# Nine shared weight buffers, and GpSimd's side work tied to the softmax's low parts

## The chip, the cores and the metric

One core of one Trainium2 chip (trn2). The metric is the device time of one execution in microseconds (us), the median of several runs. Lower is better. Five engines run their own instruction queues in order: TensorE (PE; its weight loads are PEld), VectorE (DVE), ScalarE (ACT), GpSimd (POOL) and SyncE (SP, which here only issues DMAs). They meet through semaphores.

## The reference, cut to what matters

Two layers, each "x + attention(xn) + ffn(xn)" with xn the layernorm of x; x is (2, 1024, 512) in float32.

```python
# layer 0: one head of size 128, softmax over all 1024 keys
attn = softmax(einsum('bqd,bkd->bqk', q, k) * scale);  out = (attn @ v) @ Wo + bo
# layer 0 ffn: 4 streams of 128; H_res = (1-g) I + g * sinkhorn(logits, 50 iterations)
x_mixed = einsum('btij,btjc->btic', H_res, x_streams)
y       = einsum('btnc,btn->btc', x_streams, H_pre) @ W_branch
ffn0    = x_mixed + einsum('btc,btn->btnc', y, H_post)
# layer 1: 32 heads of size 128, 8 shared K/V heads from low-rank latents, causal
q = xn @ Wq.T;  k = (xn @ Wk_down.T) @ Wk_up.T;  v = (xn @ Wv_down.T) @ Wv_up.T
attn1 = (softmax(where(causal, q @ k.T * scale, -1e9)) @ v) @ Wo.T
# layer 1 ffn: a dense product, and a low-rank one weighted by a top-2 gate over 8 experts
ffn1 = xn @ weight.T + (((xn @ lora_A) * w) @ lora_B) / 16
```

## The kernel before, in words

**Numbers.** A float32 operand is scaled and split in two float16 parts, high and low; a product is three passes of matmuls (high by high, high by low, low by high; `mm3`, `attn_out`). Weights come by a DMA that POOL issues (`fetch`) into a float32 staging tile `f2k` (four slots), and `split_pool` makes the parts with three POOL instructions: scale (L94), high part (L95), low part (L96). Products leave PSUM through `evac`: ACT writes the high part (L104), DVE the low part (L105).

**Tiles and slots.** A tile's tag names a ring of slots; a new tile waits until a slot's last reader is done. The tags that matter here: `f2k` (FB = 4), `h2k` (HB = 3), `wo` (WB = 5), `wq` (4), `P` (PB = 3, softmax rows in float32), `Phl` (LB = 3, their two parts), `PT` (3, transposed parts).

**A row step.** Layer 1 works per batch through NG = 8 groups of four heads that share one K/V head; a group has 32 row steps, each of 32 queries by four heads (128 partitions) against `QR * (s + 1)` keys. In a step (`row_step`): PE computes the scores of row s (`rows_scores`); the row before gets its reciprocal (L301) on DVE and its high part (L307) on ACT (`rows_hi`); row s gets its scaled minimum on DVE (L282, L286, the last of which is `last_row`) and its exponential on ACT (L290) (`rows_exp`); then the row before gets its **low part** on DVE (L313), a POOL memset of the part of the 128-block that causality leaves empty (L317), and one transposing DMA into `PT` (`rows_lo`). Three steps later PE multiplies by V (`group_av`), and every fourth step by Wo (`wo_block`, added into `acc` at L729). `Phl` and `P` have three slots, so a transpose that comes late holds up rows.

**What is hung on the row steps.** `layer1_attn` keeps a list `fill[(group, step)]`; `at(g, s, f)` puts work there and `put(h, s, f)` does so for the list `extra`, counted in rows from the start. Per group: K/V weights fetched at step 1 and split at 3; the four Wq weights of the next group fetched at 5, 9, 13, 17 and split two steps later; the four Wo weights of the next group fetched at 33, 35, 37, 39 and split two steps later, which is in steps 1 to 9 of that next group. During the first batch's eight groups, `extra` also holds the second batch's layer 0: its Sinkhorn chain on POOL with reciprocals on DVE (`chain_pool`, one `chain_step` for about each row from 1 to 117), its mix sums (`mix0_units`: a scaling on POOL at L613, four times four ACT scalings at L628, four POOL sums at L629), the branch (`branch0_add`, L449 and L451), its layernorm and transposes, its latents (`lat_w`, `lat_unit`), both batches' gating, and the last layer's weights (`ffn_w`, six weights, fetched and split in one go at row 212, and again at row 466 for the second batch).

**Who sets the order.** The program is traced in this order, and the Tile framework then orders each engine's queue by a simulated timeline: of the instructions that are ready there, the one traced first. Two tools bend it: `tc.issue_after(i)` and `behind(i, j)` add an edge without a semaphore: i is placed after j in the plan, but on the chip nothing waits. In the kernel before, `parts_of` places a split behind `last_row`:

```python
        hl = T(tag, [P, 2, 512], F16, bufs=bufs)
        behind(split_pool(st, hl[:, 0], hl[:, 1], scale), last_row[0])
```

Of the kernel before, what the change touches and what calls it, by code (L numbers as in the profile page):

```python
# [9 lines left out]
F16 = mybir.dt.float16  # L10
F32 = mybir.dt.float32
AF = mybir.ActivationFunctionType
ALU = mybir.AluOpType
# [3 lines left out]
P = 128  # L17
S = 1024
NB = 2
NT = S // P  # L20
# [5 lines left out]
CAPACITY = 768.0  # L26
LN_EPS = 1e-5
RMS_EPS = 1.1920929e-07
FB, HB, PB, LB, XB, WB = 4, 3, 3, 3, 4, 5
QR = 32  # L30
NR = P // QR
LG = ((0, 1, 2, 3), (4, 5, 6, 7))
# [9 lines left out]
G0, G1, GL, WT, LX, LA = 16, 200, 3, 220, 231, 240  # L42
AVD, WOD = 5, 10
KVN, QN, QNN, QH = 19, 18, 24, 1
FW, FF = 212, 221
BS, BP, BV = 4, 3, 1
CQ, CV = (0, 1), (0, 0)
PSCALE = 16384.0
# [3 lines left out]
def tile_model(ctx: ExitStack, tc: tile.TileContext, out: bass.AP, a: dict):  # L52
# [16 lines left out]
    def C(name, shape, dt=F32):  # L69
        return const.tile(shape, dt, tag=name, name=name)  # L70
# [5 lines left out]
    def bc(ap, axis, n):  # L76
        return ap.unsqueeze(axis).to_broadcast(
            [*ap.shape[:axis], n, *ap.shape[axis:]])
# [101 lines left out]


    last_pool, last_row, last_T = [None], [None], [None]
    last_hi, last_lo = [None], [None]

    def after(*insts):

# [2 lines left out]
            st.enter_context(tc.issue_after(i.ins))  # L189
        return st  # L190

    def behind(i, j):

        tc.add_manual_dep(i.ins, j.ins.name, mybir.DependencyInfo(
            mybir.DependencyClass.NoSync, mybir.DependencyReason.DATA), reason="behind")

    def rsqrt(y, ve, tag):

# [24 lines left out]
        return V.scalar_tensor_tensor(rs[:, 1, sl], mv[:, sl, 0], -1.0, rs[:, 2, sl],  # L223
                                      ALU.mult, ALU.mult)

    def normed_T(b, mv, rs, t, dst, pool, tags=(("f2k", FB), ("h2k", HB))):

        xn = T(tags[0][0], [P, NC, P], bufs=tags[0][1])
        xf = xn.rearrange("p c d -> p (c d)")
        hl = T(tags[1][0], [P, NC, 2, P], F16, bufs=tags[1][1])  # L230
        if pool > 1:
            A.activation(xf, acc[b, t], AF.Identity, scale=rs[:, 2, t:t + 1], bias=rs[:, 1, t:t + 1])
        elif pool:
            G.tensor_scalar(xf, acc[b, t], rs[:, 2, t:t + 1], rs[:, 1, t:t + 1], ALU.mult, ALU.add)
        else:
            V.tensor_scalar(xf, acc[b, t], rs[:, 2, t:t + 1], rs[:, 1, t:t + 1], ALU.mult, ALU.add)
        last_hi[0] = A.activation(hl[:, :, 0, :], xn, AF.Copy)
        eng = G if pool in (1, 2) else V
        lo = eng.tensor_tensor(hl[:, :, 1, :], xn, hl[:, :, 0, :], ALU.subtract)
        (last_pool if eng is G else last_lo)[0] = lo  # L240
        last_T[0] = nc.sync.dma_start_transpose(dst, hl.rearrange("p c l d -> p (c l d)"))
# [67 lines left out]
    def rows_lo(Pm, r, W, pool, hl, dst):  # L309
        if pool:  # L310
            G.tensor_tensor(hl[:, 1, :W], Pm[:, :W], hl[:, 0, :W], ALU.subtract)
        else:
            lo = V.scalar_tensor_tensor(hl[:, 1, :W], Pm[:, :W], r[:, 1:2], hl[:, 0, :W],  # L313
                                        ALU.mult, ALU.subtract)
        if W < hl.shape[2]:

            behind(G.memset(hl[:, :, W:], 0.0), lo)  # L317
        nc.sync.dma_start_transpose(dst, hl.rearrange("p l k -> p (l k)"))
# [32 lines left out]
    def front0(b, between=lambda: None):  # L351
        mv, rs = layernorm(b, "a")
        xT = T("xT", [P, NT, 2 * NC, P], F16, bufs=1)
        for ts in F0[b]:
            layernorm_tiles(b, mv, rs, ts)
            for t in ts:
                if b == 0:
                    tags = ("wq", 4), (("h2k", HB), ("wo", WB))[t % 2]
                    normed_T(b, mv, rs, t, xT[:, t], FP[b][t], tags)
                    if t == X1:  # L360
                        with tc.issue_after(last_T[0].ins):
                            load_x(1)
                else:
                    normed_T(b, mv, rs, t, xT[:, t], FP[b][t])
                    between()
            if b == 0 and ts[0] == 0:
                split_w0a()
# [6 lines left out]
        rf = T("rf", [P, NT], bufs=2)  # L374
        rsqrt(rf, ms, "rs")
        V.tensor_scalar(rf, rf, 1.0 / 1024.0, None, ALU.mult)
        lg = C(f"lg{b}", [P, NT, 24])
        Vh = T("V", [P, NT, 2, P], F16, bufs=2)
        for t in range(NT):
            p = PP() if t % 2 or b else srow()  # L380
# [64 lines left out]
    def branch0_add(b, t, y4, hh):  # L445

        y = y4
        y4 = T("f2k", [P, 4, P], bufs=FB)
        G.tensor_tensor(y4, bc(y, 1, 4), bc(hh[:, t, 1, :], 2, P), ALU.mult)  # L449
        af = acc[b, t]  # L450
        G.tensor_tensor(af, af, y4.rearrange("p i c -> p (i c)"), ALU.add)  # L451

# [139 lines left out]
    def mix0_units(b, t, rs, pool):  # L592


        got = {}

        def load():
            if b == 0 and t >= 4:
                if t % 2 == 0:
                    xr_more[t] = T("P", [P, 2, H], bufs=PB)  # L600
                xr = got["xr"] = xr_more[t & ~1][:, t % 2]
            else:
                xr = got["xr"] = T("xr", [P, H], bufs=XB)
            with after(t0):
                nc.sync.dma_start(xr, a["x"][(b * NT + t) * P:(b * NT + t + 1) * P, :])
            if b == 0:
                A.activation(xr, xr, AF.Identity, scale=rs[:, 2, t:t + 1], bias=rs[:, 1, t:t + 1])
                if not pool:
                    got["d"] = srow() if t < 4 else PP()
                    A.activation(got["d"], acc[b, t], AF.Copy)  # L610
                return
            with tc.issue_after(p0.ins):
                G.tensor_scalar(xr, xr, rs[:, 2, t:t + 1], rs[:, 1, t:t + 1], ALU.mult, ALU.add)  # L613

        def stream(j):
            if b == 0 and (not pool or j > 1):
                with after(*(last_rs[:1] if pool else last_rs[1:] if j else last_mix)):
                    stream_at(j)
            else:
                stream_at(j)  # L620

        def stream_at(j):
            xj = got["xr"][:, j * P:(j + 1) * P]
            by = [Hm[b][:, t, i, j:j + 1] for i in range(NC)]
            if pool:
                m = T("f2k", [P, H], bufs=FB)
                for i in range(NC):
                    A.activation(m[:, i * P:(i + 1) * P], xj, AF.Copy, scale=by[i])  # L628
                G.tensor_tensor(acc[b, t], acc[b, t], m, ALU.add)  # L629
                return  # L630

            for i in range(NC):
                sl = slice(i * P, (i + 1) * P)
                dst = acc[b, t] if j == NC - 1 else got["d"]
                last_stt[0] = V.scalar_tensor_tensor(dst[:, sl], xj, by[i], got["d"][:, sl], ALU.mult, ALU.add)

        return [load] + [lambda j=j: stream(j) for j in range(NC)]
# [30 lines left out]
    def lat_w(mc):  # L668
        st = T("f2k", [P, NC, P], bufs=FB)
        nc.gpsimd.dma_start(st, a["Wlat"][mc])  # L670
        w1 = T("h2k", [P, 2, NC, P], F16, bufs=HB)
        split_pool(st, w1[:, 0], w1[:, 1], 32.0)
        return w1

# [4 lines left out]

    def parts_of(st, tag, scale, bufs):  # L680

        hl = T(tag, [P, 2, 512], F16, bufs=bufs)
        behind(split_pool(st, hl[:, 0], hl[:, 1], scale), last_row[0])
        return hl

    def kv(b, g):
# [4 lines left out]
            got["st"] = fetch(a["Wup"][g])  # L691

        def split():
            w = parts_of(got["st"], *(("h2k", 32.0, HB) if g + b else ("wo", 32.0, WB)))
            got["w"] = w.rearrange("p l (s c d) -> p l s c d", s=2, c=2)
            got["K"] = T("K", [P, 2, S], F16, bufs=2)
            got["V"] = T("V", [P, 2, NT, P], F16, bufs=2)
# [60 lines left out]
    def layer1_attn(kv0, start, extra):  # L758
# [5 lines left out]
        def at(g, s, f):  # L764
            g, s = g + s // NS, s % NS
            fill.setdefault((g, s), []).append(f)
# [29 lines left out]
        for g in range(N):  # L796
            if g + 1 < N:
# [8 lines left out]
                for u in range(4):  # L806
                    at(g, QNN + 2 * u if new else QN + 4 * u, lambda g=g, u=u: q_unit(g + 1, u))
                for hh in range(4):
                    at(g, 33 + 2 * hh, lambda g=g, hh=hh: fetch_wo(g + 1, hh))
                    at(g, 35 + 2 * hh, lambda g=g, hh=hh: split_wo(g + 1, hh))  # L810
            for u in range(4):
                at(g, QH + (1 if (g + 1) % NG == 0 else 3) * u, lambda g=g, u=u: q_unit(g, 4 + u))
            for c in range(NT):
# [108 lines left out]

    ffw = {}

    def ffn_w():
        w = T("cmp", [P, 6, 2, H], F16, bufs=1)

        parts = [(a["WmT"][c * P:(c + 1) * P, :], 64.0) for c in range(NC)]
        parts += [(a["loraA"], 4.0), (a["loraB"], 16.0)]
        for k, (src, scale) in enumerate(parts):  # L930
            st = T("f2k", [P, H], bufs=FB)
            nc.gpsimd.dma_start(st, src)
            split_pool(st, w[:, k, 0], w[:, k, 1], scale)
            ffw["ABCDEF"[k]] = w[:, k]

    def ffn_block(b, t):
        xT = xT1[b]
# [50 lines left out]
        xT1[b] = T("xT", [P, NT, 2 * NC, P], F16, bufs=1)  # L988

    def xT_tile(b, t, pool):  # L990
        normed_T(b, *ln1[b], t, xT1[b][:, t], pool, (("f2k", FB), ("h2k", HB)) if b else
                 (("xr", XB), (("h2k", HB), ("wo", WB))[t % 2]))

    def tile_of(b, t):
        d = T("h2k", [P, 2 * NC, P], F16, bufs=HB)
        normed_T(b, *ln1[b], t, d, True, (("f2k", FB), ("xr", XB)))
        return d

# [36 lines left out]
        extra.setdefault((s // (S // QR), s % (S // QR)), []).append(f)  # L1035

    def chain_step():
        with tc.issue_after(last_row[0].ins):
            next(chain, None)

    for k in range(102):
# [36 lines left out]
    for mc in range(4):  # L1078
        put(0, LA + 2 * mc - 4, lambda mc=mc: lw.update({mc: lat_w(mc)}))
        for th in range(2):  # L1080
            put(0, LA + 2 * mc + th, lambda mc=mc, th=th: lat_unit(mc, th))
    put(0, FW, ffn_w)
    put(58, 2, ffn_w)
    for t in range(NT):
        put(0, FF + t, lambda t=t: ffn_block(0, t))
        put(60, 4 * t + 3, lambda t=t: ffn_block(1, t))
# [48 lines left out]
```

## Time and profile before

| | before |
|---|---|
| median of 3 runs | 1868.62 us (1867.13 to 1870.87) |
| the profiled execution, its own time | 1873.71 us |
| its span in the profile | 1871.6 us |
| mean granted TensorE clock | 0.971 |
| PE, DVE, ACT, POOL busy | 1724.0, 1473.9, 1198.8, 900.4 us |
| low parts (L313) | 464.5 us in 515, mean 913 ns |
| POOL memsets (L317) | 75.8 us in 384, mean 207 ns; 414.1 us idle before them for a transpose's landing |
| one Wo split on POOL, means | L94 679, L95 658, L96 1285 ns |

All of it is one execution on the chip. "Busy" is the time in which an engine has an instruction under way; a PE that is busy need not be at its peak. In the timeline a line gives start, length, engine, source line, operation, the tile written and those read, shapes, how many instructions are merged, and in brackets how long the engine was idle before it and what released it. Layer 0 takes about the first 234 us; the first batch's eight groups run from there to about 1100 us, the second batch's to the end.

### The profile page before, as it was taken

Reading aid. Unit: us, or ns where it says so; the run is one execution under the profiler, and the core shown is the slowest. Engines: PE = TensorE matmul, PEld = TensorE weight load, DVE = VectorE, ACT = ScalarE, POOL = GpSimd, SP = SyncE. Lnnn points to the kernel's source line nnn. Section 1 sums busy time; section 2 is a strip of 40 time slices with the busy share of each in tenths; the row PEclk is TensorE's granted clock in tenths of the full one; section 3 lists DMA queues with packets and bytes.
Section 4 is the critical chain, followed back from the end, with each engine's and each line's share of the span. In section 5 each row is a group of like instructions: output and inputs, shape, how many; then the busy total and the mean of one; then the engine's idle time right before and its main releaser. Section 6 shows DMA issues by size and latency. Waiting matters only on the chain. (4 is left out here: it accounts for less than half of the span.)

```text
span 1871.6 us, 34948 instructions
## 1 busy us (share of the span) xinstructions
PE 1724.0 (92%) x11458; PEld 1047.7 (56%) x11458; DVE 1473.9 (79%) x4050; ACT 1198.8 (64%) x2917; POOL 900.4 (48%) x1540
## 2 busy tenths in 40 slices
PE   4756399989999999999999999999999999999998
PEld 3333145656666566566555556566666666655665
DVE  8888977988888878787967767777777878777675
ACT  4747665657666787867535646666676767675554
POOL 5657667576857373727525332334242415155200
PEclk9887699999999999999999999999999999999999
DMA  7425234656554656477538645756565666666456
GB/s 209 91 46 112 76 66 96 149 113 133 129 127 104 150 121 152 99 146 159 134 85 154 124 101 128 131 125 146 115 143 123 137 123 141 118 143 138 89 125 119
DMA packets 707305, 230.25 MB, mean 123 GB/s; under 512 B 689953, under 2 KB 690081, under 8 KB 707122
## 3 DMA queue, kind: packets, MB, share of 16 engines
q1 hardware_dynamic: 691666, 180.75, 47.2%
q0 software_dynamic: 13152, 43.07, 8.6%
q10 hardware_dynamic: 2304, 4.20, 0.7%
q8 instruction: 90, 1.47, 0.3%
q14 instruction: 93, 0.76, 0.1%
HBM read 52.81 MB, written 4.19 MB: 30 GB/s over the span
## 5 line engine op out<-in xcount | busy, mean ns | idle before, releaser
L290 ACT ACTIVATE P<-P,nm 128x1024 f32<-128x1024 f32 (+31 forms) x528 | 391.7, 742 | 261.3 <-DVE nm L282 248.3
L313 DVE SCALAR_TENSOR_TENSOR Phl<-P,r,Phl 128x1024 f16<-128x1024 f32 (+31 forms) x515 | 464.5, 913 | 109.5 <-ACT Phl L307 104.6
L343 PE MATMUL av<-PT,V 128*128 128x256 f16 x3648 | 451.9, 275 | 18.3 <-DMA PT<-Phl 12.7
L88 PE MATMUL s<-K,Q 128*128 128x512 f16 (+22 forms) x2400 | 447.3, 319 | 22.0 <-DVE P L286 16.0
L343 PEld LDWEIGHTS <-V 128*128 128x128 f16 x3648 | 357.6, 99 | 110.4 <-issue 11.6
L307 ACT ACTIVATE Phl<-P,r 128x1024 f16<-128x1024 f32 (+31 forms) x515 | 370.2, 732 | 28.7 <-DMA PT<-Phl 12.6
L88 PE MATMUL pp<-wo,ao 128*128 128x512 f16 x1536 | 373.7, 380 | 4.6 <-ACT ao L104 3.7
L88 PE MATMUL pp<-xT,wq 128*128 128x512 f16 x1536 | 369.3, 380 | 0.9 <-DVE xr L855 0.5
L317 POOL MEMSET Phl<- 128x192 f16 (+2 forms) x384 | 75.8, 207 | 530.5 <-DMA PT<-Phl 414.1
L88 PEld LDWEIGHTS <-Q 128*128 128x128 f16 x2400 | 224.0, 99 | 180.6 <-issue 34.1
L88 PEld LDWEIGHTS <-wq 128*128 128x128 f16 x1536 | 149.6, 98 | 167.5 <-issue 3.0
L88 PEld LDWEIGHTS <-ao 128*128 128x128 f16 x1536 | 149.6, 98 | 155.6 <-ACT ao L104 5.6
L282 DVE CUSTOM_DVE_ANT_0 P<-s,mask,nm 128x272 f32<-128x272 f32 (+15 forms) x256 | 157.4, 616 | 21.2 <-PE s L88 13.3
L286 DVE TENSOR_SCALAR_CACHE_REDUCE P<-s 128x512 f32<-128x512 f32 (+15 forms) x272 | 152.4, 561 | 14.6 <-PE s L88 11.4
L302 ACT ACTIVATE r<-r 128x1 f32<-128x1 f32 x528 | 96.4, 193 | 76.2 <-DVE r L301 76.0
L104 ACT ACTIVATE ao<-av 128x512 f16<-128x512 f32 x128 | 75.4, 589 | 107.2 <-PE av L343 104.0
L301 DVE RECIPROCAL r<-r 128x1 f32<-128x1 f32 x528 | 80.7, 157 | 77.4 <-ACT P L290 73.2
L94 POOL TENSOR_SCALAR f2k<-f2k 128x512 f32<-128x512 f32 x164 | 110.3, 679 | 48.3 <-DMA f2k<-in_Wq 19.3
L729 DVE SCALAR_TENSOR_TENSOR acc<-pp,acc 128x512 f32<-128x512 f32 x128 | 86.8, 678 | 38.3 <-PE pp L88 37.9
L105 DVE SCALAR_TENSOR_TENSOR Q<-pp,Q 128x512 f16<-128x512 f32 x128 | 87.2, 681 | 31.9 <-ACT Q L104 31.8
L282 DVE CUSTOM_DVE_ANT_0 P<-s,mask 128x32 f32<-128x32 f32 (+15 forms) x256 | 104.9, 429 | 8.7 <-PE s L88 8.3
L104 ACT ACTIVATE Q<-pp 128x512 f16<-128x512 f32 x128 | 74.5, 582 | 55.1 <-PE pp L88 53.4
(262 smaller groups left out, 2113.5 us busy)
## 6 DMA issues: line engine op xcount, KB each, us to landing
f2k<-in_Wq POOLq DMA_DIRECT2D x64, 256.0 KB, 3.2
f2k<-in_WoT POOLq DMA_DIRECT2D x64, 256.0 KB, 3.3
PT<-Phl SPq DMA_TRANSPOSE x528, 3.4
acc<-in_x SPq DMA_DIRECT2D x16, 256.0 KB, 4.0
f2k<-in_Wup POOLq DMA_DIRECT2D x16, 256.0 KB, 3.6
out<-acc ACTq DMA_DIRECT2D x16, 256.0 KB, 3.7
xr<-in_x SPq DMA_DIRECT2D x12, 256.0 KB, 3.0
f2k<-in_Wlat POOLq DMA_DIRECT2D x8, 256.0 KB, 5.5
```

The source lines that it names most:

```text
L88: nc.tensor.matmul(dst, lhs(l), rhs(r), start=(i == 0 and j == 0), stop=(i == n - 1 and j == 2))
L94: first = G.tensor_scalar(stage, stage, scale, 1.0, ALU.mult, ALU.mult)
L104: A.activation(hl_hi, src, AF.Copy, scale=scale)
L105: return V.scalar_tensor_tensor(hl_lo, src, scale, hl_hi, ALU.mult, ALU.subtract)
L282: last_row[0] = V.tensor_tensor_reduce(Pm[:, o:o + w], pt[:, :w], mask[:, 512 - w:], -scale, first, ALU.add, ALU.min, nm[:, k:k + 1])
L286: last_row[0] = V.tensor_scalar(Pm[:, o:o + w], pt[:, :w], -scale, first, ALU.mult, ALU.min, accum_out=nm[:, k:k + 1])
L290: A.activation(Pm[:, :W], Pm[:, :W], AF.Exp, bias=last, scale=-1.0, accum_out=r[:, 0:1])
L302: A.activation(r[:, 1:2], r[:, 1:2], AF.Copy, scale=PSCALE)
L307: A.activation(hl[:, 0, :W], Pm[:, :W], AF.Copy, scale=r[:, 1:2])
L313: lo = V.scalar_tensor_tensor(hl[:, 1, :W], Pm[:, :W], r[:, 1:2], hl[:, 0, :W], ALU.mult, ALU.subtract)
L343: nc.tensor.matmul(p, Vh(j, l), PT(r * nj + j), start=(j == 0 and k == 0), stop=(j == nj - 1 and k == 2))
L729: V.scalar_tensor_tensor(acc[b, t], p, 1.0 / 256.0, acc[b, t], ALU.mult, ALU.add)
```

## The change

1. The tag `h2k` goes; its tiles join the tag `wo`, which now has nine slots instead of three and five. The tile `lg`, two constants before, is one slot that both batches share.
2. `last_low` remembers the newest low part on DVE (L313). `behind` can now add a real wait (a semaphore). `parts_of` (the Wq, Wo and K/V splits) uses it: a split's first instruction waits for `last_low`. So do the second batch's scaling, mix sums and branch product on POOL. `chain_step` is placed after `last_low` instead of `last_row`, without a wait.
3. The Wo weights of the next group are split at steps 22, 25, 28, 31 (at the change of batch 26, 28, 30, 32) and fetched two steps before.
4. The last layer's six weights are fetched and split one at a time, two rows apart, from row 210 and from row 466, each split behind `last_low`.

```diff
-FB, HB, PB, LB, XB, WB = 4, 3, 3, 3, 4, 5
+FB, PB, LB, XB, WB = 4, 3, 3, 4, 9
-FW, FF = 212, 221
+FW, FF = 210, 221
...
-    def behind(i, j):
-
+    def behind(i, j, wait=False):
+
+        kind = mybir.DependencyClass.Sync if wait else mybir.DependencyClass.NoSync
         tc.add_manual_dep(i.ins, j.ins.name, mybir.DependencyInfo(
-            mybir.DependencyClass.NoSync, mybir.DependencyReason.DATA), reason="behind")
+            kind, mybir.DependencyReason.DATA), reason="behind")
...
-    def normed_T(b, mv, rs, t, dst, pool, tags=(("f2k", FB), ("h2k", HB))):
+    def normed_T(b, mv, rs, t, dst, pool, tags=(("f2k", FB), ("wo", WB))):
...
                                         ALU.mult, ALU.subtract)
+            last_low[0] = lo
...
-        lg = C(f"lg{b}", [P, NT, 24])
+        lg = T("lg", [P, NT, 24], bufs=1)
...
-        G.tensor_tensor(y4, bc(y, 1, 4), bc(hh[:, t, 1, :], 2, P), ALU.mult)
+        mul = G.tensor_tensor(y4, bc(y, 1, 4), bc(hh[:, t, 1, :], 2, P), ALU.mult)
+        if b:
+            behind(mul, last_low[0], True)
...
-                G.tensor_scalar(xr, xr, rs[:, 2, t:t + 1], rs[:, 1, t:t + 1], ALU.mult, ALU.add)
+                behind(G.tensor_scalar(xr, xr, rs[:, 2, t:t + 1], rs[:, 1, t:t + 1], ALU.mult, ALU.add),
+                       last_low[0], True)
...
-                G.tensor_tensor(acc[b, t], acc[b, t], m, ALU.add)
+                add = G.tensor_tensor(acc[b, t], acc[b, t], m, ALU.add)
+                if b:
+                    behind(add, last_low[0], True)
...
-        w1 = T("h2k", [P, 2, NC, P], F16, bufs=HB)
+        w1 = T("wo", [P, 2, NC, P], F16, bufs=WB)
...
-        behind(split_pool(st, hl[:, 0], hl[:, 1], scale), last_row[0])
+        behind(split_pool(st, hl[:, 0], hl[:, 1], scale), last_low[0] or last_row[0], True)
...
-                    at(g, 33 + 2 * hh, lambda g=g, hh=hh: fetch_wo(g + 1, hh))
-                    at(g, 35 + 2 * hh, lambda g=g, hh=hh: split_wo(g + 1, hh))
+                    s = 26 + 2 * hh if new else 22 + 3 * hh
+                    at(g, s - 2, lambda g=g, hh=hh: fetch_wo(g + 1, hh))
+                    at(g, s, lambda g=g, hh=hh: split_wo(g + 1, hh))
...
-    def ffn_w():
-        w = T("cmp", [P, 6, 2, H], F16, bufs=1)
...
+    def ffn_fetch(k):
+        ffw[k] = fetch(ffw_parts[k][0])
+
+    def ffn_split(k):
+        if k == 0:
+            ffw["w"] = T("cmp", [P, 6, 2, H], F16, bufs=1)
+        w = ffw["w"][:, k]
+        behind(split_pool(ffw[k], w[:, 0], w[:, 1], ffw_parts[k][1]), last_low[0], True)
+        ffw["ABCDEF"[k]] = w
...
     def chain_step():
-        with tc.issue_after(last_row[0].ins):
+        with tc.issue_after(last_low[0].ins):
             next(chain, None)
...
-    put(0, FW, ffn_w)
-    put(58, 2, ffn_w)
+    for k in range(6):
+        for s in (FW, 8 * 58 + 2):
+            put(0, s + 2 * k - 2, lambda k=k: ffn_fetch(k))
+            put(0, s + 2 * k, lambda k=k: ffn_split(k))
```

More of the change, by code (lines that the diff above doesn't have):

```diff
@@ L182, in tile_model @@
     last_pool, last_row, last_T = [None], [None], [None]
-    last_hi, last_lo = [None], [None]
+    last_hi, last_lo, last_low = [None], [None], [None]
     def after(*insts):
@@ L357, in front0 @@
                 if b == 0:
-                    tags = ("wq", 4), (("h2k", HB), ("wo", WB))[t % 2]
+                    tags = ("wq", 4), ("wo", WB)
                     normed_T(b, mv, rs, t, xT[:, t], FP[b][t], tags)
@@ L693, in split @@
         def split():
-            w = parts_of(got["st"], *(("h2k", 32.0, HB) if g + b else ("wo", 32.0, WB)))
+            w = parts_of(got["st"], "wo", 32.0, WB)
             got["w"] = w.rearrange("p l (s c d) -> p l s c d", s=2, c=2)
@@ L923, in tile_model @@
     ffw = {}
-    def ffn_w():
-        w = T("cmp", [P, 6, 2, H], F16, bufs=1)
[L928 to L934, printed above, removed]
+    ffw_parts = [(a["WmT"][c * P:(c + 1) * P, :], 64.0) for c in range(NC)]
+    ffw_parts += [(a["loraA"], 4.0), (a["loraB"], 16.0)]
+    def ffn_fetch(k):
[6 more added lines that the diff above has]
+        ffw["ABCDEF"[k]] = w
     def ffn_block(b, t):
@@ L990, in xT_tile @@
     def xT_tile(b, t, pool):
-        normed_T(b, *ln1[b], t, xT1[b][:, t], pool, (("f2k", FB), ("h2k", HB)) if b else
-                 (("xr", XB), (("h2k", HB), ("wo", WB))[t % 2]))
+        normed_T(b, *ln1[b], t, xT1[b][:, t], pool, (("f2k", FB), ("wo", WB)) if b else
+                 (("xr", XB), ("wo", WB)))
     def tile_of(b, t):
-        d = T("h2k", [P, 2 * NC, P], F16, bufs=HB)
+        d = T("wo", [P, 2 * NC, P], F16, bufs=WB)
         normed_T(b, *ln1[b], t, d, True, (("f2k", FB), ("xr", XB)))
```

## The prediction, made before the change had run

> **What bounds the kernel now.** I read the page first, then the busy times by stretch, then TensorE's own gaps in the timeline, then what VectorE and GpSimd (POOL) did just before each gap.
>
> ```profile
> span 1871.6 us, 34948 instructions
> PE 1724.0 (92%) x11458; PEld 1047.7 (56%) x11458; DVE 1473.9 (79%) x4050; ACT 1198.8 (64%) x2917; POOL 900.4 (48%) x1540
> ```
>
> TensorE (PE) is the bound, but an average over 1871.6 us hides where it idles. The busy times by stretch (length, PE, PEld, DVE, ACT, POOL, then the granted clock) say where:
>
> ```profile
> 0.00:234.00 234.00, 132.09 (x871) 77.09 (x872) 202.05 (x644) 141.47 (x323) 150.13 (x173) 0.82 0.45 107
> 327.00:608.00 281.00, 274.95 (x1834) 170.09 (x1832) 244.56 (x694) 183.15 (x447) 192.01 (x422) 0.99 0.56 126
> 608.00:842.00 234.00, 226.92 (x1472) 138.63 (x1471) 189.14 (x486) 184.20 (x477) 120.18 (x179) 0.99 0.63 134
> 842.00:1197.00 355.00, 339.26 (x2264) 202.31 (x2262) 273.87 (x707) 208.40 (x506) 154.78 (x249) 0.99 0.60 128
> 1197.00:1684.00 487.00, 485.54 (x3216) 299.95 (x3215) 370.05 (x997) 325.77 (x798) 175.85 (x327) 1.00 0.62 130
> 1684.00:1731.00 47.00, 43.94 (x300) 27.89 (x299) 33.44 (x83) 26.24 (x54) 26.16 (x41) 0.96 0.69 138
> ```
>
> Length less PE busy: 101.9 us idle in layer 0, 6.0 + 7.1 + 15.7 in layer 1's first batch, 1.5 in most of the second, 3.1 in the stretch where the second batch's last-layer weights are split. So the second batch can't gain; layer 0 is where most idle lies, but there DVE is the busy one (202 of 234) with the unrolled Sinkhorn chain, which the change doesn't touch. The change works on 327 to 1197 and 1684 to 1731.
>
> The gaps of PE there (start, length, what; in brackets idle time and its releaser):
>
> ```profile
> 393.57 0.72 PE L88 MATMUL pp<-h2k,cmp 128*128 128x128 f16 x10 [3.58 <-DVE acc L729]
> 780.70 0.57 PE L88 MATMUL s<-K,Q 128*128 128x288 f16 x3 [2.10 <-DVE nm L282]
> 912.47 1.20 PE L88 MATMUL s<-K,Q 128*128 128x416 f16 x3 [3.91 <-DVE P L286]
> 1014.83 0.60 PE L88 MATMUL pp<-xT,h2k 128*128 128x512 f16 x2 [1.50 <-POOL h2k L95]
> 1723.76 1.65 PE L343 MATMUL av<-PT,V 128*128 128x256 f16 x7 [3.06 <-DMA PT<-Phl]
> ```
>
> Before 393.57 DVE was in one instruction, a row's low part (L313), that took 4.70 us where its kind takes 0.65, while POOL ran piece after piece:
>
> ```profile
> 388.16 4.70 DVE L313 SCALAR_TENSOR_TENSOR Phl<-P,r,Phl 128x416 f16<-128x416 f32 x1
> ```
> ```profile
> 388.62 1.15 POOL L96 TENSOR_TENSOR wo<-f2k,wo 128x512 f16<-128x512 f32 x1
> 389.75 0.61 POOL L95 TENSOR_SCALAR wo<-f2k 128x512 f16<-128x512 f32 x1
> ...
> 390.70 1.14 POOL L96 TENSOR_TENSOR wo<-f2k,wo 128x512 f16<-128x512 f32 x1
> ...
> 392.54 1.33 POOL L96 TENSOR_TENSOR wo<-f2k,wo 128x512 f16<-128x512 f32 x1
> ```
>
> That is a burst of Wo splits that had waited together for their five buffers. I sorted all 515 low parts by whether a reading POOL instruction ran beside them, and compared each with the lower quartile of its shape: 322 without are over by 0.2 us in sum, 193 with by 75 us. Low parts and POOL exclude each other. The gaps at 912.47 and 1723.76 have another root: POOL ran six last-layer splits in a row (889.7 to 912.0, and 1693.2 to 1714.1), the rows' memsets (L317) stood behind them in its queue, their transposes started late, the three Phl buffers stayed taken. Each gap is followed by a stretch at clock 0.50 (395.4, 617.3, 781.1, 910.8, 1016.6, 1723.2): 3.4 us each, 6.7 at 910.8. Half of PE's busy time in them is lost: 1.65 + 1.5 + 1.65 + 2.5 + 1.65 + 1.4 = 10.4 us.
>
> [...]
>
> **The change part by part.** The profiled execution took 1873.71 us (span 1871.6 and 2.1 around it), 5.1 over the median of 1868.62; I apply differences to the median.
>
> Gains, each as what is idle or lost at half clock there, from 0 to all of it, and what I take:
>
> *Nine buffers, Wo splits moved.* The four Wo splits of the next group go from steps 3 to 9 of that group, where K/V and Wq splits stand too, to steps 22 to 31 of the one before; with nine slots (4 + 4 + 1 live) none waits for PE (87.3 us in ten waits now). Around 376 to 399: 1.41 + 3.58 + 0.46 + 1.65 = 7.1; I take 5.5. At 1012 to 1037 the latent weights wait in the three h2k slots: 0.47 + 1.50 + 0.32 + 0.60 + 0.83 + 0.80 + 1.65 = 6.2; I take 2, since xT tiles, latents and four live Wo still share nine. From 1068 to 1202: 0.90 + 0.37 + 1.91 + 1.46 = 4.6; I take 1. In layer 0 the second batch's transposes wait for h2k (PE gaps of 0.17 + 1.01 + 0.23 + 2.24 = 3.65 from 119 to 126); I take 1, as POOL's own sums stand between. `lg` shared between batches: 0, its last reader is layer 0's start of the chain.
>
> *Mix sums, scalings and branch behind low parts.* 676 to 784: 0.94 + 0.67 + 0.32 + 2.10 + 1.65 = 5.7 (sums of 1.29 us beside lows); I take 3. 614 to 620: 1.27 + 1.27 + 1.5 = 4.0, but there 16 ACT scalings (3.91 us at 605.6) hold the exponentials; 0.5.
>
> *Last layer's weights one by one.* 872 to 917: 0.70 + 1.60 + 0.48 + 3.91 + 2.5 = 9.2; I take 5, because the Wo splits now move into the same steps (ten splits in 13 rows). 1684 to 1731: 3.06 + 1.4 = 4.5; I take 3, for the same reason.
>
> Sum taken 21; all of it 45.
>
> Costs. *The waits for readers:* a waiting split queues nothing of PE's within reach: in the twelfth group the low of row 2 ends at 1478.0, the split then takes 0.68 + 0.66 + 1.29 = 2.63 and PE reads it at 1497.2, 16 us later; Wq and Wo have ten steps or more. Zero; without that backlog it would be up to 2.6 us in each of 15 groups.
>
> *The waits for what is behind them on POOL:* memsets and the second batch's Sinkhorn chain. POOL now waits 414 us at memsets for transposes, so it runs ahead and has slack; after, it stands until the low.
>
> ```profile
> POOL Phl L317 <- DMA PT<-Phl: 414.1, 101, 11.5
> ...
> DVE sk L542 <- POOL sk L539: 11.6, 14, 2.4
> ```
>
> A chain step is three POOL pieces (0.53 + 0.35 + 0.31, or 0.55 + 0.41 + 0.35: 1.25), then a reciprocal on DVE that stands in DVE's queue ahead of rows. There are 115 lows in 234 to 608, 3.25 us a row; 102 steps over 116 rows make 3.70 us a step. Split and step need 2.63 + 1.25 = 3.88: 0.18 over, for some 33 splits 6 us of DVE waiting. If the split also stands still for a low (below), 0.84 over: 28. Below nothing too, if paced splits free the chain. I take 5, nearest the first, since DVE has 36 us idle in 327 to 608.
>
> *New overlap:* 175 lows in 487 us give 2.78 us a row with lows of 0.82 us. A split that starts at the end of a low lasts 2.63 and meets the next after 1.96: 0.67 us of overlap each, as much as an average low loses now (75/193 = 0.39) and more. So the contention isn't gone; it is capped near one piece. In the second batch PE idles 1.5 of 487 us beside it, so it costs 0 to 2 there; I take 1.
>
> Net 21 - 6 = 15: 1868.6 - 15 = 1853.6, say 1854.
>
> **The rivals.** *Slower:* the waits hold POOL in the first batch. Place: rows 1 to 117 (280 to 608), where POOL is busy 69%, and rows 200 to 224, where it has no idle time already. It decides when a split and a chain step together exceed 3.70 us, which 3.88 already does slightly. Price 28 us, plus 5 for late memsets (the two gaps of 3.06 and 3.91 less 2 that stay anyway), 33 in all; of the gains 10 remain. In full 1868.6 + 23 = 1892, at half 1868.6 + 6 = 1875; centre 1882. For it: the reciprocals do wait now (11.6 us at L542). Against: DVE's idle time covers part. *Nothing:* each gap is replaced by another nearby, as overlap per split is not smaller than now; 1865 to 1872. *More:* all bursts and their half clock go; 45 less 6 gives 1830, so 1828 to 1840. *That it doesn't do what it says:* if the scheduler had placed splits right behind lows before, the waits would be idle; but the 193 overlapped lows speak against it.
>
> **How the numbers follow.** Forecast (1840 to 1864) 0.48; more gain 0.06; nothing 0.12; slower 0.34. A measurement of this kernel can tell about 0.2%, 3.7 us: faster under 1864.9, slower over 1872.4. Faster 0.48 + 0.06 = 0.54. The range 1838 to 1884 leaves out most of the case of more gain and a third of the slower one.
>
> **What would show it.** Right: PE's gaps at about 390 and 912 and the 3.06 us near 1720 gone with their half-clock stretches; the longest L313 under 3 us; POOL no longer waiting for PE at Wo. Wrong: DVE waits for POOL at L542 and L547 well over 21 us in sum, ACT or PE waiting for Phl and PT in 280 to 608, PE busy below 485 in the second batch's 487 us, or the layer 0 stretch longer than 234 us by more than its gaps explain.

## The result and the profile after

The changed kernel takes 1856.28 us (median of 4 runs, 1854.3 to 1860.76), against 1869.74 for the kernel before on the same chip (4 runs, 1867.13 to 1872.43). The ratio is 0.9929, with a 95% interval from 0.9906 to 0.9951: 13.5 us less, where 15 was forecast. (For the experiments below the kernel before was run again beside each group; its medians there were 1868.95 to 1873.2, and each ratio is against those.)

The page of the changed kernel: span, busy time of each engine, and the group of the rows' low parts (line, engine, operation, how many, busy time and mean ns, then the idle time before them). That line is L314 now, 464.5 us before.

```profile
span 1853.7 us, 35094 instructions
PE 1715.7 (93%) x11458; PEld 1046.0 (56%) x11458; DVE 1447.6 (78%) x4050; ACT 1194.1 (64%) x2917; POOL 910.6 (49%) x1540
...
L314 DVE SCALAR_TENSOR_TENSOR Phl<-P,r,Phl 128x1024 f16<-128x1024 f32 (+31 forms) x515 | 434.4, 853 | 85.9 <-ACT Phl L308 79.5
```

PE's busy time fell by 8.3 us though its 11458 matmuls are the same. Nearly all of that is half-clock time that is gone: by the granted clock PE was busy at half clock for 54.1 us before and for 38.6 after, and half of the difference is 7.8. The low parts lost 30 us. The busy times by stretch, in the columns of the prediction (length, PE, PEld, DVE, ACT, POOL, granted clock, DMA share, GB/s):

```profile
0.00:234.00 234.00, 132.08 (x882) 77.47 (x883) 203.28 (x647) 143.43 (x327) 149.74 (x173) 0.84 0.45 107
327.00:608.00 281.00, 275.94 (x1827) 170.65 (x1825) 239.42 (x707) 182.94 (x448) 199.39 (x442) 0.99 0.59 126
608.00:842.00 234.00, 227.92 (x1512) 140.94 (x1511) 186.65 (x487) 185.63 (x501) 130.25 (x188) 1.00 0.61 133
842.00:1197.00 355.00, 339.65 (x2262) 203.06 (x2261) 267.17 (x715) 206.96 (x501) 162.05 (x254) 0.99 0.60 131
1197.00:1684.00 487.00, 487.00 (x3260) 302.35 (x3258) 363.42 (x994) 327.48 (x790) 172.10 (x317) 1.00 0.61 129
1684.00:1731.00 47.00, 47.00 (x300) 28.73 (x298) 38.02 (x92) 29.07 (x55) 30.64 (x46) 1.00 0.68 153
```

The last two rows have no idle PE left (1.5 and 3.1 us before). Since work moves across fixed borders, I also cut both executions at the same places of the program, the first low part of a group of rows: start to group 0 took 269.6 before and 265.9 after, groups 0 to 5 took 575.8 and 567.5, 6 to 8 took 351.8 and 350.5, 9 to 13 took 461.0 and 459.0, and from group 14 to the end 213.4 and 210.7. Together 18.0 us of span, which is more than the 13.5 between the medians, so some 4 to 5 us of it is chance of the two executions. Other profiles tell where.

The head: a second profile of the changed program (after2) had 269.8 there, so one profile of each can't decide. But there are nine profiles of a head with nine slots, all with the same instructions in the same order up to about 240 us (the two memset kernels below left out). They show 265.2 to 269.8 us, 266.8 in the mean. The three with the old rings show 269.6 to 271.5, 270.8 in the mean. The two sets part between 124 and 132 us, where the prediction saw the second batch's transposes wait for `h2k`. So some 4 us of the gain are most likely the slots' work in layer 0.

Groups 0 to 5: the changed order took 567.5 us in three profiles (after, after2, a_late). The order before took 575.8, but 572.9 in b_ffn (below), which has on every engine the same instructions in the same order as the kernel before up to about 880 us. So of the 8.3 us in groups 0 to 5 about 3 can be chance, and 5.4 stay. The end gave 2.7.

The waits that the change made (engine, line and what it waited for: us in total, times, longest):

```profile
POOL f2k L94 <- DVE Phl L314: 444.5, 87, 23.1
...
POOL Phl L319 <- DMA PT<-Phl: 95.7, 26, 11.4
...
DVE sk L546 <- POOL sk L543: 13.3, 21, 2.0
...
DVE sk L551 <- POOL sk L549: 11.0, 17, 1.5
```

POOL used to spend its slack at the memsets (414.1 us); now 444.5 us of it lie at the first instruction of a split, for a low part. DVE's wait for the chain hardly moved: 13.3 + 11.0 = 24.3 us, against 21.0. POOL's wait for PE at Wo (87.3 us) is gone. The gaps of PE near 390, 912 and 1720 us are gone too, but see b_ffn below for the first. PE's timeline shows two of those that are there instead (start, length, what; idle time and releaser in brackets); four more of 0.84 to 1.69 us lie between 918 and 935:

```profile
857.20 4.11 PE L88 MATMUL pp<-xT,wq 128*128 128x512 f16 x12 [3.20 <-DVE acc L737]
...
877.47 0.50 PE L88 MATMUL pp<-gw,wo 128*128 128x32 f16 x12 [2.66 <-DVE Phl L314]
```

Both stand where the first batch's last-layer weights are split, among Wo splits and dense work. From 330 us on, PE idles 28.3 us in sum (35.0 before) and runs 13.7 us at half clock (23.9): 6.7 us of idle and half of 10.2 us make 11.8, most of what these two executions differ by behind the head.

### The profile page after: what moved, and what is told of

It is laid out like the page before. It is cut to its first block, busy times and chain, and to the rows that moved or that the text cites. A ratio compares the mean times of both kernels' runs of the same rounds, so it can differ in the third digit from the quotient of the medians.

```text
span 1853.7 us, 35094 instructions
## 1 busy us (share of the span) xinstructions
PE 1715.7 (93%) x11458; PEld 1046.0 (56%) x11458; DVE 1447.6 (78%) x4050; ACT 1194.1 (64%) x2917; POOL 910.6 (49%) x1540
## 5 line engine op out<-in xcount | busy, mean ns | idle before, releaser
L314 DVE SCALAR_TENSOR_TENSOR Phl<-P,r,Phl 128x1024 f16<-128x1024 f32 (+31 forms) x515 | 434.4, 853 | 85.9 <-ACT Phl L308 79.5
L88 PE MATMUL s<-K,Q 128*128 128x512 f16 (+22 forms) x2400 | 440.7, 317 | 19.5 <-DVE P L287 11.6
L88 PE MATMUL pp<-wo,ao 128*128 128x512 f16 x1536 | 369.9, 379 | 2.9 <-ACT ao L104 2.7
L94 POOL TENSOR_SCALAR f2k<-f2k 128x512 f32<-128x512 f32 x164 | 109.5, 668 | 499.9 <-DVE Phl L314 444.5
L319 POOL MEMSET Phl<- 128x192 f16 (+2 forms) x384 | 72.6, 209 | 133.5 <-DMA PT<-Phl 95.7
```

The lines of the kernel that those rows point to most:

```text
L88: nc.tensor.matmul(dst, lhs(l), rhs(r), start=(i == 0 and j == 0), stop=(i == n - 1 and j == 2))
L94: first = G.tensor_scalar(stage, stage, scale, 1.0, ALU.mult, ALU.mult)
```

## The experiments

My theory when they began: the gain comes from fewer splits beside low parts and from bursts that no longer hold the memsets back. The rivals: the waits do nothing and it is the new places; or the slots do it. "Excess" below is what those of the 515 low parts that take longer than the lower quartile of their own shape take beyond it: 77.6 us before, 46.9 after.

**The waits alone, both ways.** In the changed kernel every new wait becomes order only (a_nowait); in the kernel before, only the waits and the chain's place are added (b_low).

```diff
a_nowait (of the changed kernel)
-        kind = mybir.DependencyClass.Sync if wait else mybir.DependencyClass.NoSync
+        kind = mybir.DependencyClass.NoSync
b_low (of the kernel before)
+            last_low[0] = lo
-        behind(split_pool(st, hl[:, 0], hl[:, 1], scale), last_row[0])
+        behind(split_pool(st, hl[:, 0], hl[:, 1], scale), last_low[0] or last_row[0], True)
...   (and the scaling, mix sums, branch and chain_step, as in the change)
```

> The changed kernel with each new semaphore turned into an edge of the plan alone: POOL's instructions are still placed after the low part, but do not wait for it. If the waits themselves keep POOL off the low parts, this gives back 5 to 9 us (1861 to 1865) and L313's busy time rises from 434 to over 450 us. Rival: buffers, moved Wo splits and single last-layer weights do it, and the waits are idle: 1854 to 1858, no more overlap than now.

> Only the waits for low parts (splits, mix sums, scalings, branch; the chain step placed after the low part); buffers, Wo steps and the weight bursts as before. By the prediction's terms (3 gained, 6 paid) 1867 to 1873, and L313's busy time falls below 450 us. Rival, that the waits do it: 1856 to 1862. Rival, that they hold POOL: over 1875, with DVE waiting longer at the chain's reciprocals.

a_nowait: 0.9933 (0.9911 to 0.9956), median 1859.1. b_low: 1.0043 (1.0028 to 1.0058), 1878.52, slower by 8 us. So in the whole change the waits are worth nothing that can be told in the time (two such intervals leave about 6 us either way), and alone they cost. They aren't idle, though. The low parts by the page of a_nowait:

```profile
L314 DVE SCALAR_TENSOR_TENSOR Phl<-P,r,Phl 128x1024 f16<-128x1024 f32 (+31 forms) x515 | 454.7, 895 | 82.0 <-ACT Phl L308 74.1
```

That is over the 450 us expected if the waits keep splits off low parts, with an excess of 66.7 us against 46.9. In its profile groups 0 to 5 took 575.1 us instead of 567.5, groups 6 to 8 took 347.3 instead of 350.5. So some 20 us of overlap came back, and the total is still not told apart.

In b_low the low parts hardly got shorter (462.4 us against 464.5), and the six last-layer weights still came as one block, now with POOL standing longer for their own transfers inside it. PE's and POOL's timelines of b_low:

```profile
1728.29 2.93 PE L345 MATMUL av<-PT,V 128*128 128x256 f16 x13 [4.42 <-DMA PT<-Phl]
```
```profile
1708.56 0.62 POOL L94 TENSOR_SCALAR f2k<-f2k 128x512 f32<-128x512 f32 x1 [3.27 <-DMA f2k<-in_loraA]
...
1719.08 0.25 POOL L319 MEMSET Phl<- 128x192 f16 x1
```

The memset at 1719.08 stood behind the block until then, and the gap that was 3.06 us is 4.42. The segment from group 14 on took 217.9 us, against 213.4; groups 6 to 8 took 3.1 us more, which I did not follow up.

**The two moves, each alone and together.** b_wo9 is nine slots and `lg` and the Wo splits at their new steps; b_ffn is the last layer's weights one by one; a_nolow is both. None has a wait for a low part.

```diff
b_wo9 (of the kernel before)
-FB, HB, PB, LB, XB, WB = 4, 3, 3, 3, 4, 5
+FB, PB, LB, XB, WB = 4, 3, 3, 4, 9
...   (tag h2k becomes wo; lg shared; the fetches move with the splits)
-                    at(g, 35 + 2 * hh, lambda g=g, hh=hh: split_wo(g + 1, hh))
+                    s = 26 + 2 * hh if new else 22 + 3 * hh
+                    at(g, s, lambda g=g, hh=hh: split_wo(g + 1, hh))
b_ffn (of the kernel before)
-    put(0, FW, ffn_w)
-    put(58, 2, ffn_w)
+    for k in range(6):
+        for s in (FW, 8 * 58 + 2):
+            put(0, s + 2 * k, lambda k=k: ffn_split(k))
...   (and the fetches; FW 212 becomes 210; ffn_split placed behind last_row)
```

> Only nine shared buffers, the shared lg and the moved Wo splits; no waits, last-layer weights in one burst. By the prediction's terms (5.5 + 2 + 1 + 1) 1859 to 1861, with the 3.58 us gap near 390 gone and both gaps of the weight bursts (3.91 and 3.06 us) still there. Rival, that the waits do it: 1866 to 1870.

> Only the last layer's weights one by one, two rows apart, placed after the row's minimum without a wait. By the prediction's terms (5 and 3) 1860 to 1863, with the gaps of 3.91 and 3.06 us gone. Rival, that the same POOL work in the same rows only moves the first of them: 1864 to 1867, the first batch's half of it unchanged and the second's gone.

> Nine buffers, moved Wo splits and the last layer's weights one by one, but nothing tied to the low parts: splits are placed after the row's minimum without a wait, mix sums, scalings and branch are free, the chain step as before. If the two parts simply add (0.9975 and 0.9962 measured each alone), 0.9937 of before, and the low parts' waits are worth nothing measurable in the whole change (0.9929). If the waits matter, 4 to 8 us more time than the change, lost in the first batch's groups 0 to 5 (575 us from the first low of group 0 to that of group 6, against 567.5).

b_wo9: 0.9975 (0.9956 to 0.9994), 1865.72. b_ffn: 0.9962 (0.9936 to 0.9987), 1862.98. a_nolow: 0.9941 (0.9917 to 0.9964), 1862.18. The first two multiply to 0.9937, so they add up, and together they are the whole change within what can be told. Against the profile of before, b_wo9 gains 4.3 us in groups 0 to 5 (and 4.3 in the head), b_ffn 4.8 in groups 6 to 8 and 4.5 at the end. b_wo9 stayed outside its forecast of 1859 to 1861. b_ffn's stretch at the end by its busy times, with PE's busy time in the second column:

```profile
1684.00:1731.00 47.00, 47.00 (x305) 29.15 (x304) 37.63 (x90) 29.80 (x59) 23.52 (x39) 1.00 0.73 147
```

The places are not quite those expected. In b_ffn the gap at the end is gone, but in PE's timeline the gap of 3.91 us at 912 is still there. In b_wo9 the 3.58 us gap is gone, but one of 4.73 stands some 16 us before its place, behind a late transpose (3.78 in a_nolow; in the changed kernel no gap over 1.3 us stands near there). PE's timelines of b_ffn and b_wo9:

```profile
911.93 0.69 PE L88 MATMUL s<-K,Q 128*128 128x416 f16 x3 [3.60 <-DVE P L286]
```
```profile
373.93 2.34 PE L345 MATMUL av<-PT,V 128*128 128x256 f16 x13 [4.73 <-DMA PT<-Phl]
```

And b_ffn is a second execution of the order before, up to 880 us. The row whose low part took 4.70 us at 388.16, and on which the gap at 393.57 hung, is there in DVE's timeline as:

```profile
389.50 0.80 DVE L313 SCALAR_TENSOR_TENSOR Phl<-P,r,Phl 128x416 f16<-128x416 f32 x1
```

PE's longest gap around it is then 0.88 us. So that long hold was in part the chance of one execution, not a fixture of the kernel.

a_nolow also shows where fewer overlaps come from. Its low parts, without one wait for them, by its page:

```profile
L314 DVE SCALAR_TENSOR_TENSOR Phl<-P,r,Phl 128x1024 f16<-128x1024 f32 (+31 forms) x515 | 436.0, 859 | 98.4 <-ACT Phl L308 82.6
```

436.0, as good as the 434.4 with all waits, and b_wo9 alone has 438.5 (b_ffn 456.3). So the moved Wo splits are enough to shorten the low parts, without a wait. That the splits of a_nowait, placed behind low parts and not waiting, overlap more again (454.7) is the plan's doing in a way that no run here separates.

**Nine slots, Wo left where it was.** b_nine is b_wo9 with the old steps.

```diff
b_nine (of b_wo9)
-                    s = 26 + 2 * hh if new else 22 + 3 * hh
-                    at(g, s, lambda g=g, hh=hh: split_wo(g + 1, hh))
+                    at(g, 35 + 2 * hh, lambda g=g, hh=hh: split_wo(g + 1, hh))
...   (and the fetches)
```

> Only the nine shared buffers and the shared lg; Wo splits at their old steps, no waits, weight bursts as before. If the buffers are what shortened layer 0 (3 to 4 us less until group 0's first low, in both kernels that have them), 1 to 3 us remain of the 5 that buffers and moved Wo splits gained together: 0.998 to 1.000. If the moved splits do all of it, 1.000 and layer 0 as before; if the buffers do all of it, 0.997.

1.011 (1.0082 to 1.0137), 1890.13: slower by some 20 us, where I had expected no change or a small gain. Groups 0 to 5 took 583.5 us (575.8 before), 6 to 8 took 367.0 (351.8); excess 95.2, half clock 34.1 us. DVE's and POOL's timelines of b_nine:

```profile
757.73 6.47 DVE L314 SCALAR_TENSOR_TENSOR Phl<-P,r,Phl 128x224 f16<-128x224 f32 x1 [0.78 <-ACT Phl L308]
```
```profile
758.05 0.61 POOL L95 TENSOR_SCALAR wo<-f2k 128x512 f16<-128x512 f32 x1
758.63 0.61 POOL L94 TENSOR_SCALAR f2k<-f2k 128x512 f32<-128x512 f32 x1
...
761.49 1.14 POOL L96 TENSOR_TENSOR wq<-f2k,wq 128x512 f16<-128x512 f32 x1
...
762.80 1.14 POOL L96 TENSOR_TENSOR wo<-f2k,wo 128x512 f16<-128x512 f32 x1
```

Wo and Wq splits now follow each other with no pause, and a low part of 0.45 us by its kind ends only with the run of them. Beside a like pile of POOL's sums and splits, from 779.78 on, three low parts took 3.83 us, and PE's timeline has a gap across them, released by the score minimum that stood behind them on DVE. It also has a longer one, in group 7, where a layernorm tile's transposes came late:

```profile
785.97 1.68 PE L88 MATMUL s<-K,Q 128*128 128x304 f16 x6 [4.57 <-DVE P L287]
...
1043.05 3.57 PE L88 MATMUL pp<-xT,wo 128*128 128x512 f16 x8 [6.95 <-DMA xT<-wo]
```

POOL's waits for PE at Wo fell from 87.3 us in ten to one of 13.8. So the wait for a slot, which I had counted as the cause of bursts, was, it seems, also a brake between them: here the splits of steps 3 to 9 run as one block. That fits groups 0 to 5, which lost 7.7 us. Most of the loss, 15.2 us, lies in groups 6 to 8, and why the transposes there are late I did not follow up. Given nine slots, moving Wo is worth 1.011 to 0.9975, 25 us; nine slots at the old steps are a loss, though the head is short here too (265.4). The moved splits with the five old slots were not run.

**Which waits matter.** Three kernels leave some of them out of the change: for mix sums, scalings and branch (a_nomix), for everything in rows 192 to 255 (a_late), for the mix sums and the branch's last sum (a_sumfree). after2 is the change itself again, as a control.

```diff
a_nomix (of the changed kernel; for all three such places)
-                       last_low[0], True)
a_late
+        wait = wait and not NW[0] <= now[0] < NW[1]
...   (NW = 192, 256; now[0] counts the rows)
a_sumfree
-                if b:
-                    behind(add, last_low[0], True)
```

> The change without the waits on the second batch's mix sums, scalings and branch; the weights' splits keep theirs. If those sums' pacing matters, groups 3 to 5 (rows 96 to 191, 283 us in the change) get 3 to 5 us longer and the time is 1859 to 1862. Rival, that they are idle: 1855 to 1858.

> The change with the waits left out (edges of the plan only) for rows 192 to 255, where POOL also makes the second batch's layernorm tiles and has no idle time. If the waits help in groups 0 to 5 but hold POOL in groups 6 and 7, the stretch from group 6's first low to group 9's falls from 350.5 to about 347 us and the time by 2 to 4 us. Rival, that these waits are idle too: no difference beyond 1 us.

> The change without the waits on the mix sums and the branch's last sum (40 of the 56 such POOL instructions are mix sums); scalings, the branch's product and the weights' splits keep theirs. In the profiles groups 2 and 3 were shortest with all waits (90.5 and 92.2 us) and groups 4 and 5 without any on the sums (91.2 and 91.4). If the two go together, 563 us from the first low of group 0 to that of group 6 and a time 3 to 7 us under the control. Rival: the differences are the plan's chance, and it lies within 2 us of the control.

> The changed kernel itself, unaltered, as the control beside the others of this call: 0.990 to 0.994 of before.

a_nomix: 0.9903 (0.9877 to 0.9929). a_late: 0.9949 (0.9929 to 0.9969), where I had expected less time and got if anything more: groups 6 to 8 took 355.8 us, not 347. a_sumfree: 0.9931 (0.9909 to 0.9953). after2: 0.993 (0.9908 to 0.9952). All four intervals overlap. I had read a_nomix as a version that beats the change; a_sumfree, most of the same edit, is not told apart from the control, so that stays unproven. a_sumfree missed its 563 us in groups 0 to 5 (566.3), so its rival, chance of the plan, is the better reading. What holds is that the waits on mix sums, scalings and branch bring no gain that can be seen. (In a_sumfree's expectation the count of sums includes the branch's.)

**What the overlap still costs.** In both kernels the split's pieces are replaced by five memsets of about the same total (2.63 us for Wo in b_memset, 525 ns each on average; 2.62 us for the three pieces before), which write but read nothing.

```diff
b_memset, a_memset (in split_pool)
+        first = G.memset(stage, 0.25)
+        G.memset(hl_hi, 0.25)
+        G.memset(hl_lo, 0.0)
+        G.memset(hl_hi, 0.25)
+        G.memset(hl_lo, 0.0)
...   (in place of the scaling, high and low part)
```

> The kernel before with each weight split's three POOL instructions replaced by five memsets of the same tiles, so that POOL reads no SBUF in them; the weights' values are thereby constants. If low parts are slowed by POOL's reads, their excess over their shapes' lower quartile falls from 78 us to under 25 us. If that slowing is what PE's gaps come from, the time falls to 1850 to 1860; if the gaps come from POOL's queue (memsets behind bursts), it stays within 5 us of before.

> The change with each weight split's three POOL instructions replaced by five memsets, so that they read no SBUF (the weights' values are thereby constants). The low parts' excess falls from 47 us to under 15. With the splits behind the low parts and Wo's slots free, POOL no longer stands at a slot with the rows' memsets behind it, so the second batch keeps its 91.8 us a group, where the kernel before with memsets lost 2 to 8 us in each; what falls in groups 0 to 5 is what overlap still costs there: 4 to 8 us, 1848 to 1853. Rival, that overlap costs nothing now: 1855 to 1858.

b_memset: 1.0103 (1.0073 to 1.0133), 1893.13. a_memset: 0.9915 (0.9887 to 0.9943), 1854.54. The excess fell to 14.1 and 15.3 us; the low parts by the page of a_memset:

```profile
L316 DVE SCALAR_TENSOR_TENSOR Phl<-P,r,Phl 128x1024 f16<-128x1024 f32 (+31 forms) x515 | 402.6, 793 | 94.4 <-ACT Phl L310 81.8
```

So in these kernels it is the splits' reading pieces that make most of the excess, 77.6 us before and 46.9 after the change, and memsets in their place leave 14.1 and 15.3. Groups 0 to 5 gained from it, 575.8 (or 572.9) to 561.7 in the one and 567.5 to 552.5 in the other, where I had expected 4 to 8 us, so after the change the splits' reading pieces still cost about 15 us there. As a whole a_memset is not told apart from the change, and its 1848 to 1853 was missed: groups 6 to 8 gave 6.2 us back (356.7) and the head had 275.1, and I did not follow these up.

b_memset met neither forecast: it lost 19 us as a whole, for another reason, in groups 9 to 13 (485.5 us, 461.0 before) and after. From its waits and its POOL and PE timelines:

```profile
POOL wq L95 <- PE pp L88: 155.3, 28, 9.7
```
```profile
1180.38 0.52 POOL L95 MEMSET wq<- 128x512 f16 x1 [7.25 <-PE pp L88]
...
1188.93 0.53 POOL L95 MEMSET wq<- 128x512 f16 x1 [2.85 <-PE pp L88]
...
1192.79 0.17 POOL L319 MEMSET Phl<- 128x64 f16 x1
```
```profile
1196.86 2.53 PE L345 MATMUL av<-PT,V 128*128 128x256 f16 x11 [5.84 <-DMA PT<-Phl]
```

POOL stood at the Wq split for slots that PE frees, 155.3 us instead of 12.6, with the rows' memsets queued behind it, and PE then waited for their transposes. In a_memset these groups took 458.0 us, though POOL stands at Wq there as well; from its waits:

```profile
POOL wq L95 <- PE pp L88: 92.3, 32, 12.3
```

So standing there is not enough for the loss. a_memset differs from b_memset in the waits, the slots and the places, and no run tells which of them spares it. The real splits without waits don't have this loss (a_nolow: 460.4).

## Why the prediction was right, and where it wasn't

The total was right, 13.5 against 15, but partly by luck, since errors offset each other: gains of 21 were forecast where the parts show about 12, and costs of 6 where none can be told.

- **Nine buffers and moved Wo, 9.5 forecast.** b_wo9 shows 0.25% of 1870, 4.7 us (interval 1.1 to 8.2). The term of 1 for layer 0 was too small: the nine-slot heads are some 4 us shorter. The term of 5.5 for the burst at 376 to 399 was too large. It was read from one execution, and in b_ffn the same row's low part takes 0.80 us in place of 4.70. b_wo9's groups 0 to 5 are 4.3 us under those of before, but 1.4 under those of b_ffn. Groups 6 to 8 gave 0.7 and groups 9 to 13 gave 0.6, where 2 and 1 were forecast.
- **The step that failed: the burst as Wo splits "that had waited together for their five buffers", with nine slots as half of the cure.** In the changed kernel none waits. In b_nine one wait is left of ten, and it is 20 us slower. With nine slots it is the new place that makes the difference, 25 us; what the new place does without them is not known.
- **Mix sums, scalings and branch, 3.5 forecast.** Nothing: a_sumfree and the control have 0.9931 and 0.993, and a_nomix without these waits is no slower. The gaps near 614 to 620 and 676 to 784 that I charged to them have partly moved; new short ones stand at 354 to 358 and at 665.
- **Weights one by one, 5 + 3 forecast.** b_ffn shows 0.38%, 7.1 us (2.4 to 12), 4.8 in groups 6 to 8 and 4.5 at the end, which is the size and nearly the places forecast, except that the gap at 912 itself stayed (3.60 us of 3.91). In the whole change the first batch's share is smaller, 1.3 us in groups 6 to 8, with the gaps at 857.20 and 877.47. I had lowered that term from 9.2 to 5 because the Wo splits move into the same steps; it should have gone lower, though that this is the reason is argued and not shown.
- **Waits, 5 + 1 forecast as cost.** The change and its control have 0.9929 and 0.993, the kernels without these waits 0.9933 (a_nowait) and 0.9941 (a_nolow): zero, within some 4 to 6 us either way. The reciprocals wait 24.3 us instead of 21.0, far from the 28 us of the slower rival. What that rival lacked is that POOL had slack to lose: 414.1 us at the memsets became 95.7, and 444.5 went to the waits. Its sign is right on the old structure, though: b_low is 8 us slower. That is not by the chain, whose waits on DVE are shorter there (17.2 us); 4.5 us of it is at the block of last-layer weights at the end, with late memsets, the place that I had priced at 5.
- **"The contention isn't gone; it is capped near one piece."** Right in the changed kernel: excess 46.9 of 77.6, longest low part 2.91 us (4.70 before). But the waits aren't needed for it (a_nolow: 49.1, also 2.91) and alone don't do it (b_low: 70.1 and 4.96), and what is left still costs about 15 us in groups 0 to 5. Nor does it hold for every kernel here: in b_nine the low part at 757.73 lost 6.02 us over a run of pieces of at most 1.14.
- **Readings that were off, without weight in the sum.** The low part that ends at 1478.0 is that of row 3, not of row 2. POOL has no idle time to speak of from 854 to 912 only; from there to row 224 it is idle for 37 of 44 us. Counting every overlap with a reading POOL instruction, 265 low parts are without and 250 with, with the same sums of excess. "Exclude each other" says more than these sums: low parts beside POOL's reading pieces are longer by 75 us in all, and with memsets in place of the pieces 14.1 and 15.3 us of excess stay.

The rival "nothing" is excluded by the interval (0.9951 is 1860.6 us, under its 1865), and "more" too (its 1840 is a ratio of 0.984).

## What to carry to other kernels

A wait for a buffer can be what keeps a queue's bursts apart (b_nine, with 13.8 us of such waits left of 87.3, is 20 us slower), so before adding slots see what runs back to back once they are there, and move that work in the same edit. When an engine runs blocks of work ahead of what others need from it, splitting the block and moving it, with the slots for it, gave all of the gain that can be told here (0.9941 of a_nolow against 0.9929); semaphores that place it finely changed where the time goes but gave nothing that can be told in the total, and on the old structure cost 8 us. Read a gap of the bound engine back to the queue that was late (here POOL's memsets behind a block), but look for it in a second execution of the same order before putting a price on it (4.70 us in one, 0.80 in the other). Price a change by part, since a right total can hide wrong terms.

## What the hardware showed that I had not expected

- One low part on DVE in b_nine took 6.02 us longer than its kind (6.47 against 0.45) beside POOL's split pieces of 0.61 to 1.14 us, with one memset of 0.25 us among them, that followed each other without a pause. It ended at 764.20, after the last of them (763.94). Such a hold need not come back: the row that was held to 4.70 us in the kernel before took 0.80 in b_ffn, with the same order of instructions on every engine.
- With the splits as memsets, which only write, the 515 low parts together were 14.1 us (b_memset) and 15.3 us (a_memset) over their own kinds' lower quartile; with the real splits 77.6 before and 46.9 after the change.
- Two executions of the same changed program differed by 3.9 us in the first 270 us and by less than 0.1 in the next 567, so an edit's effect on layer 0 can't be read from one profile of each; nine profiles against three showed it, 266.8 us against 270.8.
